# A graph attention layer on one core: a sixth pair of output tiles turned by VectorE, and the early sort, the attention's start and its shares moved

## The chip, the cores and the metric

The kernel runs on one core of a Trainium2 chip. The metric is the device time of one execution in microseconds; each kernel is run several times and the median counts. Beside the times there is one profiled execution, from which the page of the profile and all views of the trace are made.

## The reference

```python
h = jnp.maximum(_layernorm(x, axis=-1), 0.0)          # x: 2708 x 1024, fp32
q = h @ W_q.T + b_q;  k = h @ W_k.T + b_k;  v = h @ W_v.T + b_v
z = 1/sqrt(1024) * (q @ k.T)                          # 2708 x 2708
spare_z = z * adj                                     # adj: 0/1, density 0.0014771
spare_z = jnp.where(spare_z == 0.0, -10000.0, spare_z)
x = x + jax.nn.relu(jax.nn.softmax(spare_z, axis=1) @ v)
```

Each node has about four neighbours, so nearly all of the score matrix is masked.

## The kernel before

**What is computed where.** The rows are cut into 22 tiles of 128 nodes. W_q and W_k are joined into one matrix M at the start, so that a "query" row is h times M plus a bias, and a score is the product of a query row with the h row of a neighbour. While this goes on, VectorE searches the adjacency rows for the neighbours (`found`, `listed`) and ScalarE counts them (`counted`). The nodes of the first 8 tiles (the early half) and those of the others are each sorted by their number of neighbours: `counts` (L661 to L669) prepares one-hot counts, `sort` (two small matmuls L678 and L680 on TensorE, then seven VectorE operations up to `pos_i`, L689) gives each node its place, `put` (L626) scatters the table rows from GpSimd to memory, one scatter per tile, and `reload` (L638, L642) brings them back in order. From then on a tile is 128 nodes of like degree, its rows are gathered by index, and slot s of tile t is the s-th neighbour of each of its nodes.

**Units.** TensorE works through 20 units of two tiles: units 0 to 9 form the query rows (`q_results`), units 10 to 19 multiply the attention's sums with W_v (`o_results`); one tile more follows alone. A unit is a 2x2 block product by Strassen's scheme in Winograd's form: seven products of eight matmuls each instead of eight products (`multiply`, `opened`, `add_block`, L1011). In the order of TensorE these are, for unit n: s2, a12, s4, s3, then the first two products of unit n+1 (`between` and `opened`: a11 and s1), and last a22 of unit n. The block sums s1 to s4 are VectorE's (`blocks`, L722 and L742), and so are two of the four sums of the results (L1095 and L1092 for queries, L1126 and L1122 for outputs). The sum L1092 reads the same bank of PSUM into which a22 is then added; in units 4 and 5, and in the output units, ScalarE copies that bank out first (`copied`), in units 6 to 9 VectorE reads it itself. Between the products the function `after(i)`, i = 0 to 6, issues what is to run beside them; a point is written (n, i). At (n, 0) and (n, 2) the rows of unit n+1 are turned, and at (n, 4) the rows of unit n+2 are loaded.

**Turning the rows.** A product needs its rows transposed. In the ordinary way TensorE does it (`half_turned`, L415): eight transposes for the upper tile of the pair at (n, 0), eight for the lower one at (n, 2), into PSUM, from where ScalarE and VectorE take them. For output tiles in `faced_tiles` VectorE does it instead: ScalarE writes a permuted copy of the summed tile (L945), stores it (L947), SyncE brings it back in four quarters (`by_quarters`, L700), and VectorE transposes 32x32 blocks (`faces`, L705), two half tiles per tile. Which tiles are faced is decided in `sums` when a tile is done: its unit must be no later than the limit in the code, and the tile must be done before the point (unit - 2, 2). Unit 10 holds tiles 6 and 5, unit 14 tiles 17 and 13, unit 15 tiles 18 and 12, unit 19 tiles 16 and 9, and tile 8 comes alone at the end; units 19 and the last tile are always faced.

**The attention.** `attention` is a generator. It emits, tile by tile, the products of a query tile with gathered neighbour rows (`scores`, L863), the weights (`weights`, L906 to L911, with ScalarE's exponential and its first scaled row L912) and the weighted sums (`sums`, L923). Neighbour rows come by gathers of GpSimd (`gather`, L610) into 11 slots, from (10, 1) on 13; the query rows of a tile come by one gather (L612) if it is an early tile. `advance(share)` draws steps of 1.3 us from the generator at every point, so `share` sets how many attention products stand between two products of TensorE in VectorE's order. VectorE's order is written out by hand in this way all through. That of ScalarE and GpSimd is written out up to unit 4 or unit 2; after that, and on SyncE's queue, a planner puts the instructions in order by its own estimates, and `issue_after` only forbids it to put one earlier.

**Around the change.** The step codes in `steps_at` and `steps_ahead` stand for: `p` count a tile on ScalarE, `i` find, `j` list, `c` counts, `o` sort, `w` put, `b` reload, `g` a sum of squares on ScalarE. The second number of a code is a tile or a half (`c0`, `o0`: the early half). The slots are set to zero once before their first use, slots 0 to 7 by VectorE (L1261) and slots 8 to 10 by GpSimd in quarters (L1312). W_v takes the place of M in units 8 to 10: four differences of 128x2048 by VectorE (L1270) at (9, 2), (9, 4), (10, 0) and (10, 1).

Of the kernel before, what the change touches and what calls it, by code (L numbers as in the profile page):

```python
# [28 lines left out]
HIGH = 11  # L29
# [36 lines left out]
def tile_preln_masked_attention(  # L66
# [12 lines left out]
    nc = tc.nc  # L79
    N, D = x.shape  # L80
# [533 lines left out]
    rows_of = {}  # L614
    FIRST = EARLY // 2
# [147 lines left out]
    def natural_rows(n):  # L763
# [23 lines left out]
    steps_ahead = {(1, 5): "o1", (3, 6): "o0"}  # L787

    slots, free = [], []

# [128 lines left out]
    def sums(t):  # L919
        u, coef, m = us.pop(t)  # L920
        for s in range(0 if t in EMPTY else 1, K[t]):
            fill()
            chained(lambda: nc.vector.scalar_tensor_tensor(  # L923
                u, g_of[t][s], coef[:, s:s + 1], u, op0=ALU.mult, op1=ALU.add))
            free.append(g_of[t][s])
            yield 1.3
        fill()
        if t in HOSTS:
            chained(lambda: nc.vector.scalar_tensor_tensor(
                u[:HP], g_of[t][K[t]][:HP], m[:HP, 3:4], u[:HP], op0=ALU.mult, op1=ALU.add))  # L930
            free.append(g_of[t][K[t]])
            yield 1.3
            fill()
        g_of.pop(t)
        if t == SECOND:
            nc.sync.dma_start(v_dram, u)
            whole_second.append(True)
            return
        unit = next((n for n, pair in enumerate(units) if pair[0] == "o" and t in pair[1:]), len(units))
        if now < [unit - 2, 2] and unit <= len(q_pairs) + 4 or unit >= len(units) - 1:  # L940
            faced_tiles.add(t)
        print("done", t, "at", now, "unit", unit, t in faced_tiles)
        if t in faced_tiles:
            v = row_tile(f"v_{t}")
            nc.scalar.copy(v.rearrange("p (a c r) -> p c a r", a=QUADS, r=QP),  # L945
                           u.rearrange("p (c a r) -> p c a r", a=QUADS, r=QP))
            nc.scalar.dma_start(u_dram[t * P:(t + 1) * P, :], v)  # L947
        elif near(t):
            held[t] = u
        else:  # L950
            nc.sync.dma_start(u_dram[t * P:(t + 1) * P, :], u)
        done.add(t)
# [92 lines left out]
    def multiply(n, results, after):  # L1045


        X, Z = banks_of.pop(n)
        ops = ops_of.pop(n)[0]
        Y, p5 = opened_of.pop(n)  # L1050
        after(0)
        after(1)
        products.append(add_block(Y, ops["s2"], T[:, 1]))
        u2 = small("u2")
        nc.scalar.copy(u2, Y)
        after(2)
        add_block(X, ops["a12"], M[:, 1, 0])
        results[0](X)
        after(3)
        products.append(add_block(Z, ops["s4"], M[:, 1, 1]))  # L1060
        results[2](Z, u2)
        after(4)
        products.append(add_block(Y, ops["s3"], T[:, 2]))
        results[1](Y, p5)
        after(5)
        between(n)
        add_block(Y, ops["a22"], T[:, 3])
        results[3](Y)
        after(6)
# [160 lines left out]
    for n, unit in enumerate(units):  # L1230
# [4 lines left out]
            ordered.enter_context(tc.manual_schedule(engines={mybir.EngineType.DVE}))  # L1235
            nc.sync.dma_start(bp_dram, bp_sb[0:1, :])
        turn = n in (0, FIRST - 1)
        share = (20.9 if n < len(units) - 5 else 21.5) / 7
        nxt = units[n + 1] if n + 1 < len(units) else None
        if nxt is not None and nxt[0] == "o":  # L1240
            share -= 2.3 / 7 * len(set(nxt[1:]) & faced_tiles)
# [2 lines left out]
        def after(i):  # L1244
            now[1] = i
            add_due()
            if (n, i) in steps_ahead:
                follow(steps_ahead[n, i])
            if (n, i) == (2, 5):
                owe(8)  # L1250
                owe(9)
                rows_of[FIRST] = load_rows(units[FIRST])
                owe(10)
                owe(6)
                owe(7)
                rows_of[FIRST + 1] = load_rows(units[FIRST + 1])
                pooled.close()
            if n == FIRST and i in (1, 4, 5):
                for g in slots[:4] if i == 1 else slots[4:6] if i == 4 else slots[6:8]:
                    with tc.issue_after(sorted_at[-1].ins):  # L1260
                        nc.vector.memset(g, 0.0)  # L1261
            b11, b12, b21, b22 = M[:, 0, 0], M[:, 0, 1], M[:, 1, 0], M[:, 1, 1]
            for at, place, src in (((-1, 0), b12, of_wv(0, 1)), ((0, 0), b11, of_wv(0, 0)), ((0, 2), T[:, 1], of_wv(1, 1)),
                                   ((0, 3), b21, of_wv(1, 0)), ((0, 4), b22, of_wv(1, 1))):
                if (n - last_q, i) == at:
                    nc.sync.dma_start(place, src)
            for at, place, a, b in (((0, 2), T[:, 0], b12, b11), ((0, 4), T[:, 1], T[:, 1], T[:, 0]),
                                    ((1, 0), T[:, 2], b22, b12), ((1, 1), T[:, 3], b21, T[:, 1])):
                if (n - last_q, i) == at:
                    nc.vector.tensor_sub(place, a, b)  # L1270
            if (n - last_q, i) == (1, 1):
                free.extend(M.rearrange("p i j (a c) w -> p i j a (c w)", a=2)[:, 0, 1, a, :] for a in range(2))
            if (n, i) == (FIRST, 5):
                next(stream)
            if (n, i) == (FIRST, 6):
                chain.append(behind[-1])
                next(stream)
                nc.vector.tensor_tensor(bad, bad, total, op=ALU.not_equal)
            if (n, i) == (FIRST + 1, 6):
                marked(EARLY, NT)  # L1280
            if (n, i) == (FIRST + 2, 4):
                nc.vector.tensor_scalar(msq, msq, MLIMIT, None, op0=ALU.is_gt)
            if n > FIRST + 1 or n == FIRST + 1 and i > 1:
                advance(share)
            if nxt is not None:

                if i == (3 if n == 0 else 4 if turn else 0):
                    ops_of[n + 1] = blocks(*rows_of[n + 1], nc.gpsimd if n + 1 < FIRST - 1 else None)
                    with tc.issue_after(products[-1].ins) if n + 1 == FIRST else nullcontext():
                        ops_of[n + 1][1]()  # L1290
                if i == (4 if n == 0 else 5 if turn else 2):
                    ops_of[n + 1][2]()
                    rows_of.pop(n + 1)
                    if n == last_q - 1:
                        all_rows()
                if i == 3:
                    banks_of[n + 1] = banks_for(bp_sb)
                if i == 6 and n + 2 < FIRST:
                    natural_rows(n + 2)
                if i == (2 if n in (FIRST, last_q) else 4) and n + 2 > FIRST and n + 2 < len(units) and n + 2 not in rows_of:  # L1300
                    while units[n + 2][0] == "o" and not done.issuperset(units[n + 2][1:]):
                        advance(1.0)
                    rows_of[n + 2] = load_rows(units[n + 2])
            if (n, i) in steps_at:
                follow(steps_at[n, i])
            if (n, i) == (3, 4):
                searched()
            if (n, i) == (3, 6):
                for s in range(8, HIGH):
                    for c in range(0, D, D // 4):  # L1310
                        with tc.issue_after(entered[-1].ins):
                            nc.gpsimd.memset(slots[s][:, c:c + D // 4], 0.0)  # L1312
            if i == 3 and units[n - 1][0] == "o" and NT - 2 in units[n - 1][1:]:
                tail(NT - 1)
            if nxt is None and i == 1:
                uT = work.tile([P, D], FT, tag="hT", name="T_alone", bufs=2).rearrange("p (c q) -> p c q", q=P)
                faces(uT, single["rows"], 0, DC)
                single["turned"] = uT
            if n == len(units) - 2 and i == 6:
                while alone not in done:  # L1320
                    advance(1.0)
                single["rows"], = load_rows(("o", alone))
            if nxt is None and i == 3:
                single["banks"] = banks_for(bp_sb)
            if n == last_q - 1 and i == 4:

                nc.sync.dma_start(bp_sb, bv.to_broadcast([P, D]))
            if (n, i) == (last_q, 1):
                nc.vector.tensor_sub(bp_sb[:, NB:], bp_sb[:, NB:], bp_sb[:, :NB])
# [233 lines left out]
```

## Time and profile before

| what | value |
|---|---|
| median of 3 runs | 638.19 us (637.27 to 638.67) |
| the profiled execution's own time | 638.0 us |
| its span | 636.3 us, 6139 instructions |
| TensorE busy | 624.6 us, 98% |
| VectorE busy | 525.7 us, 83% |
| ScalarE busy | 283.5 us, 45% |
| GpSimd busy | 361.8 us, 57% |
| granted TensorE clock | 0.995 |

The engines are named PE (TensorE), PEld (its weight loads), DVE (VectorE), ACT (ScalarE), POOL (GpSimd) and SP (SyncE) in the rows. A row of the view in order of time has the start and the duration in us, engine, line, operation, output and inputs, how many, and in brackets how long the engine had been idle and what ended that. A row of the view by windows has the window, its length, then the busy time of PE, PEld, DVE, ACT and POOL with the number of their instructions, the granted clock, the DMA share and GB/s. A row of the waits has the waiting engine and line, what it waited for, and the sum, number and longest wait.

The units begin, by TensorE's products, at 216.2 (unit 4), 242.0 (5), 267.7 (6), 293.5 (7), 319.2 (8), 372.4 (10), 444.9 (13), 468.9 (14), 494.7 (15) and 596.1 us (19).

### The profile page before, as it was taken

The numbers are of one execution on the slowest core, as the hardware profiler recorded it, in microseconds if no ns is written. First come the engines' busy times: TensorE is split into PE (matmuls) and PEld (weight loads), VectorE is DVE, ScalarE is ACT, GpSimd is POOL, SyncE is SP. The second block draws the span as 40 slices with busy tenths as digits, with TensorE's granted clock in tenths as the row PEclk, the third lists the DMA queues.
The fourth block names the chain that finished last, engine by engine and source line by source line (L and its number), as shares of the span: only waits on it lengthen the run. The fifth ranks groups of instructions, "written<-read, shape, count | busy, mean of one in ns | idle before, by whom it ended". The sixth has DMA issues, their size and how long they took to land.

```text
span 636.3 us, 6139 instructions
## 1 busy us (share of the span) xinstructions
PE 624.6 (98%) x1627; PEld 315.5 (50%) x1627; DVE 525.7 (83%) x1021; ACT 283.5 (45%) x421; POOL 361.8 (57%) x383
## 2 busy tenths in 40 slices
PE   9999999999999999999999999999999999999994
PEld 5777766444444544444444434444444444444441
DVE  5999889897995755997889999999999989898341
ACT  3539975859667533424341243443343333422300
POOL 2649960975868277563742563576566777632431
PEclk9999999999999999999999999999999999999997
DMA  8998897598696439986699998999999999893761
GB/s 339 407 372 310 334 351 298 199 342 328 246 382 221 170 113 334 326 299 196 194 289 323 297 412 216 311 318 324 351 378 321 334 299 295 242 289 95 210 217 40
DMA packets 62352, 180.11 MB, mean 283 GB/s; under 512 B 10039, under 2 KB 17031, under 8 KB 61672
## 3 DMA queue, kind: packets, MB, share of 16 engines
q0 software_dynamic: 25136, 78.41, 39.4%
q1 hardware_dynamic: 31242, 80.19, 35.8%
q10 hardware_dynamic: 5934, 21.06, 8.5%
q8 instruction: 15, 0.25, 0.2%
q14 instruction: 25, 0.20, 0.1%
HBM read 147.23 MB, written 42.31 MB: 298 GB/s over the span
## 4 chain that ended last, share of the span: by engine, by line
PE 85%; DVE 6%; issue 4%; DMA 3%; SPq 1%; POOL 0%; ACT 0%; POOLq 0%; DVEq 0%; ACTq 0%
PE ps L1011 38%; PE psy L1011 28%; PE ps_y L476 6%; PE ps_x L476 4%; PE ps_z L476 4%; PE pt L415 3%; DVE u L923 2%; DMA g<-h_dram,tab 1%; DMA or<-u_dram 1%; DVE junk L863 1%; DVE s L722 1%; DVE wlow L1270 1%; PE ps_y L511 1%; SPq L700 1%; DVE q L1092 0%
## 5 line engine op out<-in xcount | busy, mean ns | idle before, releaser
L610 POOL DMA_INDIRECT g<-h_dram,tab x94 | 121.4, 1291 | 84.4 <-DVE u L923 31.1
L1011 PE MATMUL ps<-M,a 128*128 128x512 f32 x320 | 144.0, 593 | 0.0
L1011 PE MATMUL psy<-wlow,s 128*128 128x512 f32 x320 | 143.9, 592 | 0.0
L863 DVE SCALAR_TENSOR_TENSOR junk<-g,pq 128x1024 uint8<-128x1024 f32 x93 | 113.7, 1222 | 14.0 <-DMA g<-h_dram,tab 10.9
L1011 PEld LDWEIGHTS ps<-M,a 128*128 128x128 f32 x320 | 59.8, 190 | 70.8 <-issue 70.6
L1011 PEld LDWEIGHTS psy<-wlow,s 128*128 128x128 f32 x320 | 59.7, 190 | 70.2 <-issue 69.4
L923 DVE SCALAR_TENSOR_TENSOR u<-g,coef,u 128x1024 f32<-128x1024 f32 x69 | 88.4, 1281 | 6.9 <-ACT u L912 5.8
L389 DVE FIND_INDEX8 at<-ones,adj 128x8 uint32<-128x685 f32 (+1 forms) x88 | 74.5, 865 | 0.0
L1011 PE MATMUL psy<-wlow,a 128*128 128x512 f32 x160 | 72.0, 593 | 1.4 <-DVE q L1092 1.4
L1011 PE MATMUL ps<-M,s 128*128 128x512 f32 x160 | 72.1, 592 | 0.0
L1011 PE MATMUL ps<-wlow,s 128*128 128x512 f32 x160 | 72.0, 593 | 0.1
L368 ACT ACTIVATE sized<-adj 128x2708 uint8<-128x2708 f32 (+1 forms) x22 | 54.3, 2468 | 7.5 <-DMA adj<-in_adj_dram 6.2
L298 POOL TENSOR_TENSOR hsum<-hsum,x 128x256 f32<-128x256 f32 (+1 forms) x56 | 38.7, 729 | 25.6 <-DVE wlow L444 21.2
L1110 POOL DMA_INDIRECT y<-in_x_dram,tab x19 | 34.8, 1832 | 29.1 <-ACT y L1127 15.9
L1011 PEld LDWEIGHTS psy<-wlow,a 128*128 128x128 f32 x160 | 30.3, 190 | 40.0 <-issue 37.1
L1011 PEld LDWEIGHTS ps<-wlow,s 128*128 128x128 f32 x160 | 30.3, 190 | 38.6 <-issue 37.9
L1011 PEld LDWEIGHTS ps<-M,s 128*128 128x128 f32 x160 | 30.3, 190 | 38.1 <-issue 37.4
L912 ACT ACTIVATE u<-g,coef 128x1024 f32<-128x1024 f32 x18 | 20.7, 1147 | 32.1 <-DVE coef L911 32.1
L808 POOL DMA_INDIRECT out_dram<-y,tab x21 | 25.0, 1188 | 16.4 <-DVE flag L1354 6.1
L626 POOL DMA_INDIRECT tab_dram<-tab,pos_i x22 | 21.9, 995 | 20.7 <-DVE pos_i L689 15.3
L276 ACT ACTIVATE x<-x,r 128x1024 f32<-128x1024 f32 (+1 forms) x22 | 25.9, 1235 | 7.3 <-POOL r L266 7.3
L760 ACT COPY ps<-bp_sb 128x512 f32<-128x512 f32 x42 | 24.5, 595 | 7.2 <-DVE y L1145 6.7
(251 smaller groups left out, 843.5 us busy)
## 6 DMA issues: line engine op xcount, KB each, us to landing
adj<-in_adj_dram SPq DMA_DIRECT2D x21, 1354.0 KB, 11.3
x<-in_x_dram SPq DMA_DIRECT2D x21, 512.0 KB, 3.9
h_dram<-x ACTq DMA_DIRECT2D x21, 512.0 KB, 8.7
u_dram<-v ACTq DMA_DIRECT2D x13, 512.0 KB, 6.4
or<-u_dram SPq DMA_DIRECT2D x52, 128.0 KB, 7.0
q_late<-q SPq DMA_DIRECT2D x12, 512.0 KB, 6.0
pq<-q_late SPq DMA_DIRECT2D x12, 512.0 KB, 8.6
M<-in_wv_dram SPq DMA_DIRECT2D x4, 1024.0 KB
```

The source lines that it names most:

```text
L276: nc.scalar.activation(xs[i][:n], xs[i][:n], AF.Relu, bias=r[:n, 4, i:i + 1], scale=r[:n, 3, i:i + 1])
L298: small.append(nc.gpsimd.tensor_add(hsum[:n, cols], hsum[:n, cols], xt[:n, cols]))
L368: nc.scalar.activation(sized[:n], a[:n, :, :PW], AF.Abs, accum_out=total[:n, t:t + 1])
L389: nc.vector.max_index(at[:n, k - first_k, g, :], ones[:n, 0:8], a[:n, g, :])
L476: mm = nc.tensor.matmul(bank, a_tile(o + H * a[0], a[1], i), b(o), start=first and o == 0, stop=(o == H - 1), skip_group_check=True)
L610: return nc.gpsimd.indirect_dma_start(out=dst, out_offset=None, in_=src, in_offset=off, bounds_check=N - 1, oob_is_err=False)
L760: nc.scalar.copy(return_[h], row[:, h * NB:(h + 1) * NB])
L808: to = nc.gpsimd.indirect_dma_start(out=out, out_offset=bass.IndirectOffsetOnAxis(ap=ptab.bitcast(U32)[:n, t, SLOTS:SLOTS + 1], axis=0), i ...
L863: chained(lambda: nc.vector.scalar_tensor_tensor(junk, g_of[t][s], 1.0, tq[t], op0=ALU.mult, op1=ALU.mult, accum_out=zall[:, t, s:s + 1]))
L923: chained(lambda: nc.vector.scalar_tensor_tensor(u, g_of[t][s], coef[:, s:s + 1], u, op0=ALU.mult, op1=ALU.add))
L1011: mm = nc.tensor.matmul(bank, a[:, c, :], b[:, c, :], start=False, stop=(c == 3), skip_group_check=True)
L1110: return nc.gpsimd.indirect_dma_start(out=y[:n], out_offset=None, in_=x, in_offset=off, compute_op=ALU.add)
```

## The change

It does six things.

- The limit for faced tiles goes from unit 14 to unit 15, so that the pair 18 and 12 can be turned by VectorE too.
- The last listing and the counts of the early half go from (3, 5) to (3, 3); the early sort goes from the end of unit 3 to the place before its last product.
- GpSimd no longer zeroes slots 8 to 10; VectorE zeroes slots 4 to 6 at (4, 4) and 7 to 10 at (4, 5).
- The row gathers of unit 6, asked for at (4, 2), may not be issued before the last put of the early half.
- The attention is drawn from (5, 0) on, in place of (5, 2).
- The share of a unit is 21.2 us up to unit 7, 19.4 in units 8 to 10 and 20.9 in units 11 to 14, in place of 20.9 in all of these. It stays 21.5 after that. As before, 2.3 us are taken off for each faced tile of the next unit.

```diff
-                (3, 1): "i21", (3, 3): "p21", (3, 5): "j21 c0 g0", (3, 6): "w0-7 g1 g2 g3 g4", (4, 4): "b0"}
-    steps_ahead = {(1, 5): "o1", (3, 6): "o0"}
+                (3, 1): "i21", (3, 3): "p21 j21 c0", (3, 5): "g0", (3, 6): "w0-7 g1 g2 g3 g4", (4, 4): "b0"}
+    steps_ahead = {(1, 5): "o1"}
...
-        if now < [unit - 2, 2] and unit <= len(q_pairs) + 4 or unit >= len(units) - 1:
+        if now < [unit - 2, 2] and unit <= len(q_pairs) + 5 or unit >= len(units) - 1:
             faced_tiles.add(t)
...
         after(5)
         between(n)
+        if n == FIRST - 1:
+            follow("o0")
         add_block(Y, ops["a22"], T[:, 3])
...
-        share = (20.9 if n < len(units) - 5 else 21.5) / 7
+        share = (21.2 if n < last_q - 1 else 19.4 if n < last_q + 2 else 20.9 if n < len(units) - 5 else 21.5) / 7
...
-                for g in slots[:4] if i == 1 else slots[4:6] if i == 4 else slots[6:8]:
+                for g in slots[:4] if i == 1 else slots[4:7] if i == 4 else slots[7:]:
...
-            if n > FIRST + 1 or n == FIRST + 1 and i > 1:
+            if n > FIRST:
                 advance(share)
...
-                    rows_of[n + 2] = load_rows(units[n + 2])
+                    with tc.issue_after(entered[-1].ins) if n == FIRST else nullcontext():
+                        rows_of[n + 2] = load_rows(units[n + 2])
...
-            if (n, i) == (3, 6):
-                for s in range(8, HIGH):
-                    for c in range(0, D, D // 4):
-                        with tc.issue_after(entered[-1].ins):
-                            nc.gpsimd.memset(slots[s][:, c:c + D // 4], 0.0)
```

## The prediction

> **What bounds the kernel now.** I read the page's busy shares, then TensorE's waits, then the chain of waits, then VectorE, GpSimd and SyncE in order of time around the places that the diff touches.
>
> ```profile
> span 636.3 us, 6139 instructions
> PE 624.6 (98%) x1627; PEld 315.5 (50%) x1627; DVE 525.7 (83%) x1021; ACT 283.5 (45%) x421; POOL 361.8 (57%) x383
> PE psy L1011 <- DVE q L1092: 1.4, 1, 1.4
> 372.40:396.80 24.40, 24.34 (x58) 10.63 (x57) 22.70 (x45) 10.00 (x18) 10.05 (x6) 1.00 0.90 290
> 420.90:444.90 24.00, 24.00 (x57) 10.61 (x57) 23.48 (x41) 8.21 (x15) 16.73 (x13) 1.00 1.05 335
> 468.94 0.87 PE pt L415 x8
> 469.82 3.44 PE psy L1011 x8
> 473.25 0.87 PE pt L415 x8
> 568.65 6.87 PE psy L1011 x16
> ```
>
> TensorE is busy in 98% of the span and works without a gap from unit to unit; a product is eight matmuls and 3.44 us. So time is won only by taking work off TensorE or by removing one of its few waits. It has one wait in the units, 1.4 us, for VectorE's sum of a query pair (L1092), and unit 10, the first output unit, takes 24.40 us where a like unit takes 24.00. The last four rows show what a turned pair costs it: two groups of eight transposes, 0.87 us each, between products, while at 568.65, at the same place of unit 18, whose successor's rows VectorE turns, sixteen matmuls follow each other. VectorE is the engine behind: in unit 12 it is busy 23.48 of 24.00 us.
>
> **The sixth pair.** Counting the steps of 1.3 us that the shares draw from the attention, tile 12, the later one of unit 15, is summed at point 5 of unit 12, ahead of the limit at point 2 of unit 13, so both tiles qualify. TensorE loses both groups in unit 14: 2 x 0.87 = 1.74 us. VectorE gets four half transposes.
>
> ```profile
> L705 DVE STREAM_TRANSPOSE a<-or x18: 667/704/711, 346.1 to 580.8; 128x512 f32<-128x512 f32 x18
> 447.23 1.30 DVE L705 STREAM_TRANSPOSE a<-or 128x512 f32<-128x512 f32 x2
> 452.68 0.71 DVE L705 STREAM_TRANSPOSE a<-or 128x512 f32<-128x512 f32 x1 [0.49 <-DMA or<-u_dram]
> 460.53 0.25 SPq L1130 DMA_DIRECT2D tail_dram<-y  x1
> 460.85 0.80 SPq L1212 DMA_DIRECT2D or<-u_dram  x2
> L700 SPq DMA_DIRECT2D or<-u_dram x52: 302/430/802, 325.5 to 599.1; - x52
> DMA to landing us min/median/max: 3.1/7.0/15.1
> ```
>
> Four times 0.70 is 2.8 us on VectorE; the share of unit 14 is cut by 4.6 us for it, three attention products fewer, which units 16 and 17 take up (17 each in place of 16). ScalarE gets two copies more and loses three; it is 45% busy, I cost that at nothing. SyncE now issues eight quarter loads at 0.43 us in place of two loads, behind the tail's store at 460.53: by the median of 7.0 us the first tile's four land at about 469.6, the second's at 471.3. VectorE came to these steps 2.3 and 7.8 us into unit 13 (447.23 and 452.68, from 444.9), so it will want them at about 471.2 and 476.7, counted from unit 14's 468.94: hidden. But they can be later, unit 14's quarters already kept it 0.49 us; the far end is the 15.1 us, a rival below. The Trainium skill (VectorE: DVE Perf Modes, section Rules for kernel authors) would do the opposite: 128x128 transposes on TensorE where PSUM as destination is fine. By it the sum would be without the 1.74 us; it weighs the instruction alone, and here the rows show a full TensorE, so I do not follow it.
>
> **The early counts, sort and reload.**
>
> ```profile
> 200.65 0.69 DVE L1095 TENSOR_TENSOR q<-ps,u 128x512 f32<-128x512 f32 x1 [2.36 <-issue]
> 208.49 0.28 DVE L402 TENSOR_TENSOR cand<-first,at 128x128 f32<-128x128 f32 x1
> 212.64 0.59 ACT L1027 COPY p<-ps 128x512 f32<-128x512 f32 x1 [2.86 <-PE ps L1011]
> 212.99 0.22 DVE L669 TENSOR_SCALAR tab<-keys 128x128 uint32<-128x128 f32 x1
> 215.88 0.23 PE L678 MATMUL ps_in<-sort,before 128*128 128x144 bf16 x1
> 218.97 1.01 POOL L626 DMA_INDIRECT tab_dram<-tab,pos_i  x1 [11.57 <-DVE pos_i L689]
> 228.16 0.97 POOL L626 DMA_INDIRECT tab_dram<-tab,pos_i  x1 [0.30 <-issue]
> 229.13 3.12 POOL L1312 MEMSET g<- 128x256 f32 x12
> 230.36 0.38 SPq L638 DMA_DIRECT2D tab<-tab_dram  x1
> 233.40 0.99 POOL L612 DMA_INDIRECT pq<-q_dram,tab  x1 [1.15 <-DMA tab<-tab_dram]
> 244.21 0.95 POOL L612 DMA_INDIRECT pq<-q_dram,tab  x1 [0.30 <-issue]
> ```
>
> Listing and counts (208.49 to 213.2, 4.7 us) move into the gap that ends at 200.65. They push unit 3's sum L1095 from 200.65 to about 203; its bank is next wanted two products later, and so is that of L1092 behind it: no cost. The sort's matmuls need the counts, then long done, so they go from 215.88 to 212.7, 3.2 us sooner, and the eight puts and SyncE's reload with them. The two row gathers that are now held behind the puts take 2 x 1.3 us of GpSimd in the time in which it waits for the reload; the 3.12 us of memsets go to VectorE as three memsets at 0.91 us ahead of its first gathered row, where it waited 5.10 us (below). So the query of tile 6 is gathered at about 230.2, that of tile 5, behind seven row gathers, at 241.0 in place of 244.21. TensorE gains nothing here directly.
>
> **Attention sooner and the new shares.**
>
> ```profile
> 240.41 1.22 DVE L863 SCALAR_TENSOR_TENSOR junk<-g,pq 128x1024 uint8<-128x1024 f32 x1 [5.10 <-DMA g<-h_dram,tab]
> 251.16 1.23 DVE L863 SCALAR_TENSOR_TENSOR junk<-g,pq 128x1024 uint8<-128x1024 f32 x1 [1.10 <-DMA pq<-q_dram,tab]
> 254.65 0.15 DVE L906 SCALAR_TENSOR_TENSOR w<-w,keys 128x3 f32<-128x3 f32 x1
> 255.18 1.22 DVE L863 SCALAR_TENSOR_TENSOR junk<-g,pq 128x1024 uint8<-128x1024 f32 x1
> 247.40 1.28 DVE L722 TENSOR_TENSOR s<-a,pt 128x512 f32<-128x512 f32 x2 [3.23 <-ACT a L718]
> 283.26 0.69 DVE L1092 TENSOR_TENSOR q<-psy,p 128x512 f32<-128x512 f32 x1 [0.25 <-PE psy L1011]
> 350.98 1.28 DVE L923 SCALAR_TENSOR_TENSOR u<-g,coef,u 128x1024 f32<-128x1024 f32 x1 [1.35 <-ACT u L912]
> 363.37 2.28 DVE L1270 TENSOR_TENSOR wlow<-wlow 128x2048 f32<-128x2048 f32 x1
> 368.08 0.68 DVE L1092 TENSOR_TENSOR q<-psy,p 128x512 f32<-128x512 f32 x1
> ```
>
> Unit 5 now emits 16 attention products in place of 11. Ahead of L1092 of units 6, 7, 8 and 9 stand 27, 42, 57 and 69 products; before it was 22, 37, 53 and 66. VectorE runs in order, so this puts L1092 later wherever it cannot begin sooner. It can by about 3 us: tile 5's query lands at 248.0 (251.16 less 3.2). From there to L1092 of unit 6: 24 products at 1.27 (between the 1.22 and 1.28 of the rows, with the read of the accumulator) = 30.5, four tiles' weights at 0.5 (254.65 to 255.18) 2.0, two sets of four block sums (L722) 5.1, three sums 1.8, together 39.4 us: it starts at 287.4 and ends at 288.0. In units 6 to 9 TensorE's last product of the unit waits for that read of the bank; at 283.26 VectorE came just as the product was there, and two products (6.87 us) lie between, so the limit is 290.1. That leaves 2.1 us, no wait. From 288.0 to L1092 of unit 9: 42 products 53.3, weights 1.5, three waits for ScalarE's first row (1.35 each) 3.9, two block sums 5.1, four transposes with their four sums 5.3, two W_v differences 4.5, five sums and the bias 3.7: 77.3, so it ends at about 366 without a wait for a gather, 367.5 with one or two. The limit there is the present end less the wait, 368.76 - 1.4 = 367.4. So the 1.4 us goes, or up to 1 us of it stays; I take back 0.3. Unit 10 has two products fewer (10 for 12) and loses its 0.4 us.
>
> **The end.**
>
> ```profile
> 591.14 1.27 DVE L929 SCALAR_TENSOR_TENSOR u<-g,m,u 64x1024 f32<-64x1024 f32 x1
> 605.03 1.25 DVE L705 STREAM_TRANSPOSE T_alone<-or 128x1024 f32<-128x1024 f32 x1 [11.56 <-DMA or<-u_dram]
> 609.69 3.60 PE L1011 MATMUL ps<-M,T_alone 128*128 128x512 f32 x8
> ```
>
> The last tile is summed at 592.4, comes back through memory and is turned by 606.3; TensorE wants it at 609.7. With TensorE some 3 us sooner and VectorE carrying one product more behind unit 14, these 3.4 us shrink to about 1. I take 0.3 us for it as the mean of nothing and a small wait.
>
> **Sum.** -1.74 (transposes) - 1.4 + 0.3 (unit 9) - 0.4 (unit 10) + 0.3 (end) = -2.9 us against the profiled execution's own 638.0 us (span 636.3 and 1.7 us around it), 635.1. The median of the runs shown is 638.19, 0.2 us above it; I put the forecast on the runs' side and give the unseen small waits 0.3 us: 635.6 us.
>
> **The rivals.**
>
> (a) *VectorE's lag eats it.* The 2.1 us at unit 6 and the half us at unit 9 are small beside a gather's spread. If tile 5's query lands at 250 to 252 in place of 248.0, up to 2 us of wait appear in unit 6; that, or unit 9's wait kept whole, or both give 636.7 to 638.7. For it: the 1.10 us of waiting for just this query; against it: the queue in front of it is 3 us sooner by rows that are fixed. It comes out within 0.2% of now (1.3 us, about what a measurement of this kernel can tell from no change).
>
> (b) *The row gathers get ahead of the queries, slower.* If the row gathers now held behind the puts, and those of the next unit, stand in GpSimd's queue before the queries, four at 1.3 us, the queries come from 233.4 + 5.2, and tile 5's lands at 256.4: L1092 of unit 6 is ready at 296.4 against 290.1, 6.3 us of TensorE waiting, 638.0 - 3.2 + 6.3 = 641. It makes the kernel slower once that query lands after about 254.6 (250.1, the 3.2 us gained and 1.3). Against it: the next unit's rows are asked for a unit later, and their buffers are then taken.
>
> (c) *The quarter loads of unit 15 are late, slower.* At 15.1 us the first tile's land at 477.7, 6.5 us after VectorE comes to them. TensorE does not stop there (it wants the block sums four products later), but the attention then ends 6.5 us later with 1 us of cover left at the end: 635.1 + 5.5 = 640.6, slower from a delay of about 5 us on. For it: the 0.49 us above; against it: the median of 7.0. The Trainium skill's advice above would come true in this way.
>
> (d) *The sixth pair does not qualify*, its tile being summed too late. Then the 1.74 us goes: 637.3. The limit has four points of margin in the count, so hardly.
>
> **How the numbers follow.** Forecast 0.56; (a) 0.20, within 0.2%; (b) 0.12 and (c) 0.09, slower; (d) 0.03, within 0.2%. Faster 0.56, same 0.23, slower 0.21. The forecast's own range is 634.3 (all of 1.74, 1.4 and 0.4 from 638.0 and nothing taken back gives 634.5) to 636.9. The range for 8 in 10 takes in (a), (d) and the lower parts of (b) and (c): 634.3 to 639.2.
>
> **What would show it.** Right: 16 transposes (L415) fewer, unit 14 at 24.0 us in place of 25.8; four half transposes (L705) more; the first put near 215.8 and tile 5's first product near 248; no TensorE wait for L1092 over 0.5 us; the last transposed tile ready before its product. Wrong: a wait of TensorE for L1092 in unit 6 or 7; VectorE waiting for `or` in unit 14 by more than 2 us; the last product chain waiting for T_alone.

## The result, and the profile after

The changed kernel takes 647.34 us (median of six runs, 644.91 to 649.77) against 638.26 us for the kernel before on the same chip: 1.0142 times as long, interval 1.0113 to 1.0171. It is slower by 9 us where 2.6 us less was forecast. The profiled execution took 644.91 us, 6.9 us more than that of before. It is the fastest of the six (granted clocks 0.994 in it, 0.987 to 0.992 in the others), so some 2 us of the 9 are in no trace.

Two lines of the page of the changed kernel, then TensorE's waits:

```profile
span 643.2 us, 6114 instructions
PE 624.8 (97%) x1611; PEld 314.2 (49%) x1611; DVE 531.2 (83%) x1028; ACT 284.3 (44%) x420; POOL 363.1 (56%) x371
```

```profile
PE psy L1011 <- ACT u L1055: 5.7, 2, 4.4
PE pt L415 <- DMA qr<-h_dram,tab: 2.5, 1, 2.5
PE ps_y L511 <- POOL hsum L121: 1.2, 1, 1.2
```

Sixteen matmuls fewer, as the change says, and the 1.4 us of waiting for VectorE's sum q is gone. In its place stand two waits for a copy by ScalarE (`u2` in the code, `u` in the rows, L1055) and one for gathered rows; the wait at L511 is at the kernel's start and was there before. (The sum's line L1092 is L1094 here, L1095 is L1097, L1270 is L1272; L1055 and those ahead of it keep their numbers.) The windows of the changed kernel that differ, units 5, 6, 10 and 14:

```profile
241.95:269.40 27.45, 26.13 (x73) 11.99 (x71) 19.42 (x37) 9.46 (x17) 16.04 (x15) 1.00 0.80 274
269.40:297.90 28.50, 25.98 (x75) 12.51 (x75) 26.25 (x45) 9.92 (x16) 18.73 (x14) 1.00 0.89 300
375.40:405.60 30.20, 25.79 (x57) 11.09 (x56) 22.86 (x40) 9.62 (x17) 8.32 (x6) 0.94 0.70 227
477.70:501.76 24.06, 24.06 (x59) 10.62 (x58) 23.47 (x40) 6.42 (x11) 19.06 (x15) 1.00 1.05 317
```

The other units with transposes take 25.8 us here too, so units 5 and 6 lose 1.7 and 2.7 us. Unit 10 takes 30.20 us in place of 24.40 (5.8 more), unit 14 takes 24.06 in place of 25.8 (1.74 less), and unit 9 is 1.4 us shorter without its wait: 1.7 + 2.7 + 5.8 - 1.74 - 1.4 = 7.1, measured 6.9.

**Unit 5**, the changed kernel's rows in order of time, all engines:

```profile
242.82 0.95 POOL L612 DMA_INDIRECT pq<-q_dram,tab  x1 [0.30 <-PE pt L415]
250.60 1.23 DVE L863 SCALAR_TENSOR_TENSOR junk<-g,pq 128x1024 uint8<-128x1024 f32 x1 [7.68 <-issue]
253.73 1.15 ACT L912 ACTIVATE u<-g,coef 128x1024 f32<-128x1024 f32 x1 [8.63 <-issue]
254.79 0.56 ACT L1055 COPY u<-psy 128x512 f32<-128x512 f32 x1
255.41 3.70 PE L1011 MATMUL psy<-wlow,s 128*128 128x512 f32 x8 [1.32 <-ACT u L1055]
```

VectorE stands 7.68 us in front of tile 5's first product. The row names no releaser, but the gather of tile 5's query, issued at 242.82, landed 7.7 us later, at 250.5. (In the kernel with the shares undone, below, the same wait, of 9.0 us there, is put down to this gather by name.) The products of tile 5 are in its order ahead of tile 6's weights, ScalarE's first row of tile 6 (L912) waits for these weights, and the copy L1055, for which TensorE waits, stands behind L912 in ScalarE's queue. GpSimd hands on the same wait; first the changed kernel, then before:

```profile
256.32 0.94 POOL L612 DMA_INDIRECT pq<-q_dram,tab  x1 [6.13 <-DVE junk L863]
263.99 0.95 POOL L612 DMA_INDIRECT qr<-h_dram,tab  x1 [0.30 <-issue]
271.93 1.06 PE L415 MATMUL pt<-ident,qr 128*128 128x128 f32 x8 [2.52 <-DMA qr<-h_dram,tab]
```

```profile
251.92 1.29 POOL L612 DMA_INDIRECT qr<-h_dram,tab  x1 [0.30 <-issue]
257.94 0.94 POOL L612 DMA_INDIRECT pq<-q_dram,tab  x1 [3.46 <-DVE junk L863]
```

The gather of a later query, which waits for VectorE to be done with a buffer, has moved ahead of the gathers of unit 7's rows `qr`. These go out 12 us later than before (263.99 against 251.92), and TensorE waits for them.

**Unit 10** of the changed kernel, and the granted clock (column behind the five engines) in the stretch behind the wait:

```profile
358.09 3.78 SPq L1268 DMA_DIRECT2D M<-in_wv_dram  x2
367.03 6.58 SPq L833 DMA_DIRECT2D pq<-q_late  x2
381.90 1.23 DVE L863 SCALAR_TENSOR_TENSOR junk<-g,pq 128x1024 uint8<-128x1024 f32 x1 [7.28 <-DMA pq<-q_late]
387.06 0.30 ACT L898 ACTIVATE w<-w,m 128x3 f32<-128x3 f32 x1 [9.70 <-DVE m L897]
388.25 1.15 ACT L903 ACTIVATE u<-hsum,m 128x1024 f32<-128x1024 f32 x1 [0.81 <-DVE m L902]
389.31 0.56 ACT L1055 COPY u<-psy 128x512 f32<-128x512 f32 x1
389.93 5.40 PE L1011 MATMUL psy<-wlow,s 128*128 128x512 f32 x8 [4.41 <-ACT u L1055]
```

```profile
389.93:395.40 5.47, 5.47 (x9) 2.40 (x10) 5.43 (x6) 1.33 (x4) 1.18 (x1) 0.69 0.27 65
```

The same chain again: VectorE waits 7.28 us for tile 17's query (asked for at 367.03, landed 14.8 us later), tile 7's weights (L898, L903) come late, and in ScalarE's queue they stand ahead of the copy for which TensorE waits. TensorE waits 4.41 us, and the eight matmuls behind it take 5.40 us at a clock of 0.69, against 3.6 to 3.7 elsewhere: 1.8 us more. Before, the copy of unit 10 was through long before tile 7's weights:

```profile
379.96 0.58 ACT L1055 COPY u<-psy 128x512 f32<-128x512 f32 x1
385.34 0.30 ACT L898 ACTIVATE w<-w,m 128x3 f32<-128x3 f32 x1 [3.67 <-DVE m L897]
```

### The profile page after: what moved, and what is told of

The parts are those of the page before. It is cut to its first block, busy times and chain, and to the rows that moved or that the text cites. A ratio compares the mean times of both kernels' runs of the same rounds, so it can differ in the third digit from the quotient of the medians.

```text
span 643.2 us, 6114 instructions
## 1 busy us (share of the span) xinstructions
PE 624.8 (97%) x1611; PEld 314.2 (49%) x1611; DVE 531.2 (83%) x1028; ACT 284.3 (44%) x420; POOL 363.1 (56%) x371
## 4 chain that ended last, share of the span: by engine, by line
PE 79%; DMA 7%; issue 7%; DVE 4%; POOL 2%; ACT 1%; POOLq 0%; DVEq 0%
PE ps L1011 35%; PE psy L1011 25%; PE ps_y L476 6%; PE ps_x L476 4%; PE ps_z L476 4%; PE pt L415 3%; DMA pq<-q_late 2%; POOL g L610 1%; DVE junk L863 1%; DVE u L923 1%; DMA g<-h_dram,tab 1%; DMA qr<-h_dram,tab 1%; DMA v_dram<-u 1%; DMA wlow<-in_wq_dram 1%; DVE wlow L1272 0%
## 5 line engine op out<-in xcount | busy, mean ns | idle before, releaser
L610 POOL DMA_INDIRECT g<-h_dram,tab x94 | 124.4, 1323 | 78.5 <-DVE u L923 31.0
L1011 PE MATMUL psy<-wlow,s 128*128 128x512 f32 x320 | 145.8, 599 | 5.7 <-ACT u L1055 5.7
L1011 PE MATMUL ps<-M,a 128*128 128x512 f32 x320 | 144.0, 593 | 0.0
L863 DVE SCALAR_TENSOR_TENSOR junk<-g,pq 128x1024 uint8<-128x1024 f32 x93 | 113.6, 1221 | 24.5 <-DMA pq<-q_late 10.2
L1011 PEld LDWEIGHTS psy<-wlow,s 128*128 128x128 f32 x320 | 60.2, 192 | 77.8 <-issue 70.0
L1011 PEld LDWEIGHTS ps<-M,a 128*128 128x128 f32 x320 | 59.9, 190 | 71.3 <-issue 70.3
L1011 PE MATMUL psy<-wlow,a 128*128 128x512 f32 x160 | 72.0, 593 | 0.0
L1011 PE MATMUL ps<-M,s 128*128 128x512 f32 x160 | 71.9, 592 | 0.0
L1011 PE MATMUL ps<-wlow,s 128*128 128x512 f32 x160 | 71.9, 592 | 0.0
L1011 PEld LDWEIGHTS ps<-wlow,s 128*128 128x128 f32 x160 | 30.4, 190 | 38.3 <-issue 37.3
L1011 PEld LDWEIGHTS ps<-M,s 128*128 128x128 f32 x160 | 30.3, 190 | 38.1 <-issue 36.9
L1011 PEld LDWEIGHTS psy<-wlow,a 128*128 128x128 f32 x160 | 30.2, 190 | 37.9 <-issue 36.1
L912 ACT ACTIVATE u<-g,coef 128x1024 f32<-128x1024 f32 x18 | 20.7, 1148 | 36.1 <-DVE coef L911 22.8
L808 POOL DMA_INDIRECT out_dram<-y,tab x21 | 26.4, 1259 | 11.7 <-issue 4.9
L945 ACT COPY v<-u 128x1024 f32<-128x1024 f32 x15 | 15.7, 1045 | 38.6 <-DVE u L923 31.8
```

The costliest lines, as they stand in the source:

```text
L610: return nc.gpsimd.indirect_dma_start(out=dst, out_offset=None, in_=src, in_offset=off, bounds_check=N - 1, oob_is_err=False)
L808: to = nc.gpsimd.indirect_dma_start(out=out, out_offset=bass.IndirectOffsetOnAxis(ap=ptab.bitcast(U32)[:n, t, SLOTS:SLOTS + 1], axis=0), i ...
L863: chained(lambda: nc.vector.scalar_tensor_tensor(junk, g_of[t][s], 1.0, tq[t], op0=ALU.mult, op1=ALU.mult, accum_out=zall[:, t, s:s + 1]))
L1011: mm = nc.tensor.matmul(bank, a[:, c, :], b[:, c, :], start=False, stop=(c == 3), skip_group_check=True)
```

## The experiments

Theory 1: the earlier start of the attention does it. Its form 1a says: through ScalarE's queue order alone. Its form 1b says: because VectorE is led to data that isn't there yet, whichever engine carries that on. Theory 2: the new shares do it. Theory 3: the transfers of unit 10 come late, beside W_v's loads. Chips differ by up to 0.4% (the kernel before took 638.0, 638.5, 640.1 and 640.7 us on the four used), so ratios to the kernel before on the same chip are compared. On the last two chips TensorE also waits 1.1 to 2.6 us for `qr` at 202 to 205 us, in all kernels profiled there; that is left aside.

**One part undone, one part alone**

```
e1 (changed kernel)   - if n > FIRST:                  advance(share)
                      + if n > FIRST + 1 or n == FIRST + 1 and i > 1:
e2 (changed kernel)   - share = (21.2 ... 19.4 ... 20.9 ... 21.5) / 7
                      + share = (20.9 if n < len(units) - 5 else 21.5) / 7
e3 (changed kernel)   both of these
e4 (kernel before)    - unit <= len(q_pairs) + 4
                      + unit <= len(q_pairs) + 5
```

Start undone:

> Changed kernel with one thing undone: the attention begins at point 2 of unit 5 again; early counts, sort, sixth pair and new shares stay. Theory 1 (the earlier start puts tile 6's row and tile 7's weights ahead of TensorE's copies in ScalarE's queue, and the copies then wait with VectorE for a query): L1055 of units 5 and 10 stand ahead of them again, so TensorE's 5.7 us of waiting for ScalarE's u goes and unit 10 takes 24 to 25 us; 635 to 637.5 us. Theory 2 (the new shares do it): the waits stay, 643 to 646 us. Theory 3 (only the late query of tile 17, loaded beside W_v): the wait in unit 10 stays, that of unit 5 goes, 640 to 642 us.

Shares undone:

> Changed kernel with only the shares of the attention undone (20.9 and 21.5 sevenths again); the attention begins at point 0 of unit 5. Theory 1 (the earlier start): the wait in unit 5 stays, and that of unit 10 too, since tile 7's weights still stand ahead of its copy; 643 to 648 us. Theory 2 (the shares): 635 to 638 us. Theory 3 (the late query of tile 17): the wait of unit 5 stays or goes with the rest, that of unit 10 stays where this query is loaded beside W_v still; 640 to 646 us.

Both undone:

> Changed kernel with both the start of the attention and the shares undone; what is left is the sixth pair, the early counts, sort and reload, and the memsets on VectorE. Theories 1 and 2: no wait for ScalarE's u in units 5 and 10; the sixth pair's 1.74 us is won and unit 9's wait of 1.4 us for L1092 may stay: 635 to 637 us. If the early sort and reload are themselves the trouble (row gathers behind the query gathers on GpSimd): a wait for qr at unit 6 stays, 639 to 642 us.

Sixth pair alone:

> Kernel before with one thing of the change: VectorE turns the sixth output pair. All theories: unit 14 takes 24.0 us in place of 25.8 and nothing else moves, 1.74 us less than the kernel before, 636 to 637 us. If VectorE has no room for four half transposes more, the end or unit 14 gives it back: 638 to 640 us.

Measured: start undone 638.22 us, 1.0000 [0.9985, 1.0014]; shares undone 645.02 us, 1.0103 [1.0080, 1.0126]; both undone 639.89 us, 1.0020 [1.0000, 1.0040]; sixth pair alone 641.03 us, 1.0041 [1.0026, 1.0057]. With the shares undone the waits stay, so theory 2 falls as the main cause (the 0.4% by which that kernel lies below the changed one may be the shares', or the spread; the intervals meet). With the start undone the waits of units 5, 6 and 10 are gone, so theory 1 stands, and late transfers alone don't make unit 10's wait. But the time is no better than before, above the 637.5 expected; with both undone it missed the 637 as well. In the run with the start undone, TensorE's largest wait and what leads to it:

```profile
593.53 1.27 DVE L929 SCALAR_TENSOR_TENSOR u<-g,m,u 64x1024 f32<-64x1024 f32 x1
608.52 1.25 DVE L705 STREAM_TRANSPOSE T_alone<-or 128x1024 f32<-128x1024 f32 x1 [12.66 <-DMA or<-u_dram]
609.82 3.70 PE L1011 MATMUL ps<-M,T_alone 128*128 128x512 f32 x8 [2.50 <-DVE T_alone L705]
```

The last sum comes 2.4 us later than before (591.14), the transposed tile 3.5 us later, and TensorE, now earlier, waits 2.50 us. The sixth pair alone was expected at 636 to 637 and came out slower than before, beyond the 638 to 640 of its other case too. In it:

```profile
461.89 5.09 SPq L700 DMA_DIRECT2D or<-u_dram  x8
477.74 1.30 DVE L705 STREAM_TRANSPOSE a<-or 128x512 f32<-128x512 f32 x2 [6.97 <-DMA pq<-q_late]
493.78 5.39 PE L1011 MATMUL psy<-wlow,a 128*128 128x512 f32 x8 [3.04 <-ACT taken L1076]
```

The quarter loads go out at 461.89 and VectorE turns their tile at 477.74, 15.9 us later, after an idle 6.97 us. (The row puts the wait down to a query load. But the quarters landed only 12.5 to 17.1 us after their issue, median 14.4, with the DMA engines at a share of 1.07 from 461.89 to 477.74.) TensorE loses 3.04 us and the clock. With both undone it is the same wait with 5.91 us; with the start alone undone it doesn't appear. And L1092's wait of 1.3 us stays with the sixth pair alone and is gone with both undone: the early sort, with the moved memsets and held gathers, is enough to remove it, without the earlier start.

**What carries the waits**

```
e5   - nc.scalar.activation(u, g_of[t][0], AF.Copy, scale=coef[:, 0:1])
     + if t == 6: chained(lambda: nc.vector.tensor_scalar(u, g_of[t][0], coef[:, 0:1], None, op0=ALU.mult))   (else as before)
e6   + unit 10: nothing at points 0 and 1, three shares at point 2
e8   start undone (as e1) and  - unit <= len(q_pairs) + 5   + unit <= len(q_pairs) + 4
e9   - unit <= len(q_pairs) + 5   + unit <= len(q_pairs) + 4
```

Tile 6's row on VectorE:

> Changed kernel with one instruction moved: the first row of tile 6 is scaled by VectorE (1.3 us of its own time more) and not by ScalarE (L912, 1.15 us). All else stays, the early start too, and VectorE still waits for tile 5's query. Theory 1a (ScalarE's queue order carries VectorE's wait to TensorE): TensorE's 1.3 us of waiting for u in unit 5 goes, that of 4.4 us in unit 10 stays; 642.5 to 644.5 us. Theory 1b (the early start costs through VectorE's own lateness, or through the gathers, and ScalarE's order is beside the point): the wait in unit 5 comes back under another name, sum or transposed rows; 644.5 to 647 us.

Unit 10's steps later:

> Changed kernel with the attention steps of points 0 and 1 of unit 10 emitted at its point 2, so that tile 7's two weights (L898, L903) stand behind TensorE's copy L1055 of that unit in ScalarE's queue. VectorE's order of products is the same, and it still waits for tile 17's query. Theory 1a (ScalarE's order): the wait of 4.4 us for u in unit 10 goes, and with it the 1.8 us by which the eight matmuls behind it are longer; unit 5 and unit 6 as in the changed kernel; 637.5 to 640 us. Theory 1b (VectorE's lateness): TensorE waits in unit 10 or 11 for another thing of VectorE's, 642 to 646 us.

Start and sixth pair undone:

> Changed kernel with two things undone: the attention begins at point 2 of unit 5 again, and five output pairs are turned by VectorE, not six. Left are the early counts, sort and reload and the new shares. If the sixth pair's 2.8 us on VectorE are what makes the end wait 2.5 us for T_alone in the run with the start alone undone: no wait there, TensorE's transposes of unit 14 back (1.74 us), the 1.4 us for L1092 gone; 636 to 637 us. If the end's wait comes of the shares or the longer way of the last tile through memory: the wait stays, 638.5 to 640 us.

Sixth pair undone:

> Changed kernel with the sixth pair alone undone (five pairs turned by VectorE); the early start stays. All theories: the waits of units 5, 6 and 10 stay, since they lie before unit 14. If the sixth pair gains TensorE 1.74 us and nothing takes it back while the end has cover: 1.7 us more than the changed kernel, 646.5 to 648.5 us. If it gives back at the end what it gains: as the changed kernel, 644 to 646 us.

Measured: tile 6's row on VectorE 651.30 us, 1.0184 [1.0161, 1.0207]; unit 10's steps later 648.68 us, 1.0149 [1.0127, 1.0171]; start and sixth pair undone 636.54 us, 0.9964 [0.9950, 0.9979]; sixth pair undone 653.39 us, 1.0206 [1.0168, 1.0245]. TensorE's waits with tile 6's row on VectorE (three lines longer, so L1011 is L1014 and L1055 is L1058), then with unit 10's steps later:

```profile
PE psy L1014 <- ACT u L1058: 6.3, 1, 6.3
PE pt L415 <- DMA qr<-h_dram,tab: 5.2, 1, 5.2
```

```profile
PE ps L1011 <- ACT taken L1078: 4.9, 1, 4.9
PE pt L415 <- DMA qr<-h_dram,tab: 3.3, 1, 3.3
PE psy L1011 <- DVE wlow L1272: 1.9, 1, 1.9
PE psy L1011 <- ACT u L1055: 1.1, 1, 1.1
```

Both are longer than either form of theory 1 expected. The wait that was aimed at goes each time, and others come or grow. With tile 6's row moved, unit 5's 1.3 us are gone and the wait for `qr` grows from 2.5 to 5.2 us. With unit 10's steps later, its 4.4 us for `u` are gone, and waits for W_v's difference (1.9) and for another copy (4.9) come; the 1.1 us are unit 5's. So form 1a falls. (In the first kernel unit 10's own wait was 6.3 us too, in place of 4.4, which the moved row doesn't explain.) ScalarE only carries the wait; VectorE's idle time in front of a missing query (in unit 10 of these two 9.1 and 9.2 us) is what TensorE sees, through whichever engine comes first. The sixth pair undone beside the early start lengthened the kernel by 0.6% (1.0206 against 1.0142), 4 us and not 1.7. Its wait in unit 10 was 6.4 us that time, ahead of anything that the sixth pair touches, so I put the rest down to the spread of these waits between chips and runs; no run shows where it comes from.

With start and sixth pair undone TensorE has no wait over 0.31 us after 200 us, and the transposed last tile (605.31 to 606.56, for a product at 608.64) is there in time: that version came out as expected, and is faster than the kernel before by 0.36%. It differs from the one with the start alone undone by the sixth pair only, which therefore costs 0.36% there, some 2.3 us; 2.50 less 1.74 are 0.8 of them, the rest is in no row that I can name.

**How far ahead, and the end**

```
e10  - if n > FIRST:          + if n > FIRST and (n, i) not in ((last_q, 5), (last_q, 6)):
e11  start undone, and        + if (n, i) in ((FIRST + 2, 0), (FIRST + 2, 1)): advance(share)
e12  start undone, and        + if not (t == 16 and s in (1, 2)):   (around the weighted row)
e13  (kernel before)          - if n > FIRST + 1 or n == FIRST + 1 and i > 1:   + if n > FIRST:
```

Given back in unit 9:

> Changed kernel with the early start kept, but the attention passes over points 5 and 6 of unit 9, so that from there on it is no further than it was with the later start. Theory 1b (VectorE is led to a query that isn't there yet; what stands behind it in VectorE's order, W_v's differences, reaches TensorE late by whichever engine): in unit 10 W_v's second difference stands ahead of tile 17's first product again, VectorE's wait of 7 to 9 us for that query goes, and TensorE's in unit 10 too; the waits of units 5 and 6 (about 4 us) stay; 638.5 to 641.5 us. Theory 3 (the query of tile 17 comes late of itself, beside W_v's loads): unit 10 still waits, 643 to 647 us.

Begun later, caught up in unit 6:

> Changed kernel with the attention beginning at point 2 of unit 5 again, but two shares drawn at each of points 0 and 1 of unit 6, so that from unit 6 on it stands as far ahead as in the changed kernel. Theory 1b: no wait in unit 5, and that for transposed rows in unit 6 goes or shrinks under 1 us; unit 10 waits as in the changed kernel, 4 to 6 us with what the clock adds; 641 to 645 us. If the start itself is what costs, and not the place of the attention in unit 10: 636 to 638.5 us.

Two rows left out:

> The kernel with the start of the attention alone undone, and in it two of tile 16's weighted rows left out of VectorE's sums (2.56 us of its time in the last units); all else in place, so the output lacks them. If VectorE's load behind unit 14, with the sixth pair's 2.8 us, is what makes the end wait for T_alone: the wait of 2.5 us goes, 634.5 to 636.5 us, 1.5 to 2.5 us less than the same kernel with them. If it is the last tile's way through memory: the wait stays, 637.5 to 639 us.

The start alone:

> Kernel before with one thing of the change: the attention begins at point 0 of unit 5. There the search's sort and the queries are not a product sooner, so tile 5's query lands at about 251 us and more. Theory 1b: waits in units 5 and 6 of at least the changed kernel's 4 us and one of 4 to 8 us in unit 10, 646 to 652 us. If the early start costs only with the rest of the change: 637 to 640 us.

Measured: given back in unit 9 651.62 us, 1.0190 [1.0124, 1.0256]; begun later and caught up 647.48 us, 1.0107 [1.0068, 1.0146]; two rows left out 637.66 us, 0.9964 [0.9944, 0.9984]; the start alone 652.11 us, 1.0166 [1.0121, 1.0210]. TensorE in unit 10 where the attention begins later and catches up; then VectorE there where it gives back two points in unit 9:

```profile
391.75 5.29 PE L1011 MATMUL psy<-wlow,s 128*128 128x512 f32 x8 [6.94 <-ACT u L1055]
```

```profile
382.44 2.29 DVE L1272 TENSOR_TENSOR wlow<-M 128x2048 f32<-128x2048 f32 x1 [7.15 <-DMA M<-in_wv_dram]
```

The first settles that the lead itself costs: no wait in units 5 and 6, and yet 1.07% in all, nearly all of it from unit 10 (of 638 us, 644.8, within what 1b expected). VectorE waited 9.8 us for tile 17's query there. The second missed its numbers (638.5 to 641.5). The lead was given back, tile 17's product stands behind W_v's difference again, and TensorE's longest wait in unit 10 fell to 1.2 us; but now VectorE waits 7.15 us for W_v itself, and the steps that were put off are missed at the end (TensorE waits 2.9 us for T_alone). A query and a weight late by the same 7 us pointed to the transfers, not to the order. The start alone in the kernel before costs 1.7% (of 638 us, 648.6, in the range of theory 1b): it needs nothing else of the change. Its waits were each shorter than 1b named, 2.96 and 0.81 us in units 5 and 6 and 3.42 us in unit 10, but the first and the last lowered the clock.

With two of tile 16's weighted rows left out, 2.56 us of VectorE, the end's wait is gone (T_alone at 606.88 for a product at 609.05), and the ratio falls from 1.0000 to 0.9964, some 2.3 us. Counted back from the moment at which TensorE is ready for that product, the last sum comes 2.55 us sooner than in the kernel with the start alone undone (592.71 before 609.05, against 593.53 before 607.32), the time that was left out. So VectorE's work in the last units sets the end there.

**The transfers in unit 10**

```
e14 (changed kernel), e15 (start undone)   + if t not in (17, 13):   gathered.append(gather(...))
```

Fewer transfers, early start:

> Changed kernel with the eight row gathers of tiles 17 and 13 left out (4 MB that would move at 340 to 385 us, so the output lacks their rows); all engines' other work and its order stay, the early start too. Theory 3 (the DMA engines are full there, so tile 17's query and W_v's parts land 15 us after their issue): the query lands 10 us or less after it, VectorE's wait for it falls under 3 us and TensorE's in unit 10 under 1.5 us; units 5 and 6 as in the changed kernel; about 5 us less than the changed kernel, 639 to 642 us where the kernel before takes 638. Theory 1b alone (the query is asked for too soon after its product, full engines or not): VectorE's wait stays over 5 us and TensorE's over 3 us; 643 to 647 us.

The control:

> The kernel with the start of the attention alone undone, and the same eight row gathers left out: the control. There TensorE waits for nothing at 340 to 385 us, so fewer transfers should gain nothing but, at the end, up to 2.5 us where VectorE is a little sooner: 635.5 to 638.5 us where the kernel before takes 638, by both theories.

Measured: 645.18 us, 1.0059 [1.0038, 1.0079], and the control 640.91 us, 1.0001 [0.9979, 1.0024], as without the leaving out (1.0000). Both lie where theory 3 had them (of 638 us, 641.8 and 638.1). The windows (the last two columns are the DMA engines' share and GB/s) of the changed kernel, then of it with fewer transfers, which runs 5.9 us behind it there, and in that the query's load and VectorE's product with it (one line more, so L863 is L864):

```profile
365.00:375.00 10.00, 10.00 (x24) 4.37 (x23) 8.95 (x18) 3.97 (x7) 6.76 (x3) 1.00 1.03 373
375.00:385.00 10.00, 10.00 (x25) 4.37 (x23) 3.10 (x3) 1.87 (x3) 0.88 (x1) 1.00 0.89 361
```

```profile
375.00:385.00 10.00, 10.00 (x25) 4.50 (x24) 9.33 (x23) 4.23 (x7) 2.62 (x2) 1.00 0.62 213
```

```profile
372.91 6.58 SPq L833 DMA_DIRECT2D pq<-q_late  x2
380.42 1.22 DVE L864 SCALAR_TENSOR_TENSOR junk<-g,pq 128x1024 uint8<-128x1024 f32 x1
```

The same two rows in the kernel before:

```profile
373.84 14.16 SPq L833 DMA_DIRECT2D pq<-q_late  x3
382.29 1.22 DVE L863 SCALAR_TENSOR_TENSOR junk<-g,pq 128x1024 uint8<-128x1024 f32 x1
```

With fewer transfers the order is the same, VectorE doesn't wait, the query is there within 7.5 us in place of 14.8, and TensorE waits for nothing in unit 10: 0.83% less than the changed kernel, 5.3 us. The kernel before asks for that query at 373.84 and uses it at 382.29 without a wait. The changed kernel asks 6.8 us sooner and has it at 381.8, so the earlier request won at most 0.5 us. So unit 10's loss comes of an attention that is led, by its lead, into a stretch in which the DMA engines are full with W_v, rows and queries. The Trainium skill (DMA: Bandwidth & Descriptors, section Issuing engines are not separate DMA queues) says that transfers issued by the scalar, sync and gpsimd engines run on the same 16 DMA engines and interleave; the trace agrees, since leaving out GpSimd's gathers halved the landing of SyncE's load. What is left, 0.6%, I put down to units 5 and 6, whose waits were still 1.7 and 2.3 us, the second with a clock of 0.77 behind it. Asking for tile 17's query ahead of W_v's loads was not tried, nor was gathering tile 5's query ahead of the row gathers that stand before it.

## Why the prediction was wrong, step by step

- **The sixth pair, -1.74.** Right for TensorE: 1611 matmuls in place of 1627, unit 14 at 24.06 us. The quarter loads, a rival in the prediction (c), were in time in the changed kernel and late in the kernel with the sixth pair alone: 15.9 us from issue to use, near the 15.1 named, for 4.8 us (641.0 against 638.0 less 1.74) of the 5.5 named. The price came by another way than (c) had it: as a wait at unit 14's last product (3.04 us) and the clock behind it, more than at the end.
- **The early counts, sort and reload.** Right in kind, sizes short: the query of tile 6 is gathered at 232.08 (230.2 expected), that of tile 5 at 242.82 (241.0), and VectorE's product with it begins at 250.60 (248.0): the gather was 1.8 us later than expected, and landed in 7.7 us in place of the 7.0 that were taken over from before.
- **Attention sooner.** This is the step that failed. It asked one question, when L1092 comes, and answered it rightly: 38.5 us from tile 5's first product to that sum of unit 6 (39.4 reckoned), and no wait for it in any unit. (Its three waits of 1.35 us each make 4.05 and not 3.9, which changes nothing.) It didn't ask which data the lead reaches, and what else stands behind VectorE while it waits for them. In unit 5 that is a query that comes 7.7 us after VectorE stands before it; in unit 10, tile 17's query among full DMA engines. "Unit 10 has two products fewer (10 for 12) and loses its 0.4 us" became 5.8 us more. Nor did it look at the queues that carry such a wait: ScalarE's, judged by its 45% of busy time, and, but for rival (b), GpSimd's. It let VectorE begin tile 5 at 248.0 itself. Tile 6's products end at 242.9, so some 5 us of standing were in its own plan, at no price. The quoted row of unit 10 had a DMA share of 0.90, and was read for TensorE's 0.4 us alone.
- **Unit 9, -1.4 + 0.3.** Came true, but the earlier start wasn't needed: with both undone the wait is gone as well, and the earlier start alone, in the kernel before, leaves 0.7 us of it.
- **The end, +0.3.** Mis-sized: in the changed kernel the stalls ahead hide it, but with the start undone it is 2.5 us. The 2.8 us of transposes were rightly counted on VectorE, and then let go as "nothing and a small wait". By it alone, -1.74 + 2.5, the sixth pair doesn't pay.
- **Rival (a)** had the condition right (the query at 250 to 252) but put its wait at L1092 in unit 6 and its price at 2 us; it came at L1055 in unit 5 and at `qr` in unit 6 and cost 4.4. **Rival (b)** had the queues of GpSimd in mind, the wrong way round: here the queries got ahead of the row gathers.

## What to carry to other kernels

When work is moved forward in an order that is fixed beforehand, list for each of its first steps when its data lands; where the data isn't sooner, the engine only stands, and everything behind it in its order and in the queues of the engines that wait for it comes later. A load asked for sooner in a stretch where the DMA engines are full may land hardly sooner (here 0.5 us at most for 6.8). And an engine with 83% of busy time can still set the end: work moved to it late in the kernel is paid there, unless the end has that much cover.

## What the runs showed of the hardware

A TensorE wait of little more than 2 us can cost its length nearly twice (2.26 us of waiting, and 1.7 us more for the products behind it). Eight 128x512 matmuls behind a wait took 3.7 us, or 5.3 to 6.7; in the kernel with the shares undone, and in that with two points given back:

```profile
256.38 5.40 PE L1011 MATMUL psy<-wlow,s 128*128 128x512 f32 x8 [2.26 <-ACT u L1055]
622.01 3.70 PE L1011 MATMUL ps<-M,T_alone 128*128 128x512 f32 x8 [2.87 <-DVE T_alone L705]
```

The granted clock over these two rows was 0.68 and 1.00. Ahead of products, every wait under 2 us left the clock alone and every one of 3.4 us or more lowered it; between 2.26 and 3.04 us both happened. Ahead of the shorter transposes, 2.33 us lowered it in one kernel and 3.30 us left it alone in another. The Trainium skill (TensorE: Matmul & The Clock Gate, section Why this matters for your kernels) advises no idle gaps over about 3 us; here 2.26 us was enough once, so the measurement is the stricter. Why one wait lowers the clock and a longer one doesn't was not tried.
